# Norm scale and offset applied in the copy out of PSUM instead of being folded into the next weights

## The chip, the cores and the metric

The kernel runs on one core of one Trainium2 chip. The time is device microseconds of one execution; the time before is the median of three runs, 3001.75 us (2999.12 to 3003.61). A profile was taken of one further execution, whose own time was 3113.44 us and whose span from the first to the last instruction was 3111.6 us. All durations below come from that profiled execution, which is 3.7% longer than the runs.

Engine names in the profile: PE is the matrix engine, PEld its weight loads, DVE the vector engine, ACT the scalar (activation) engine, POOL the engine that issues the indirect DMAs (gathers and scatters of rows), SP the engine that issues plain DMAs.

## The reference

Eight graphs share one sparse adjacency matrix of 2048 nodes (a node has about 16 neighbours). Each node has 128 features. Four layers run one after the other. Layers 0 and 1 are transformer layers with attention over the neighbours; layers 2 and 3 are graph attention (GAT) layers. Cut to what matters:

```python
# layers 0 and 1
Q, K, V = h @ Wq, h @ Wk, h @ Wv
attn = softmax(where(adj == 0, -inf, Q @ K.T / sqrt(16)))      # per head, 8 heads of 16
x = layer_norm(h + attn @ V @ Wo + bo) * ln1_g + ln1_b
y = relu(x @ W1 + b1) @ W2 + b2
x = layer_norm(x + y) * ln2_g + ln2_b
# layers 2 and 3
h = x @ W
e = leaky_relu(h @ a_src [rows] + h @ a_dst [columns], 0.2)
x = layer_norm(softmax(where(adj == 0, -inf, e)) @ h + x) * ln_gamma + ln_beta
```

Every layer norm has a scale (g) and an offset (b) of 128 numbers each.

## The kernel before

**Tiling and stages.** Nodes are sorted by their number of neighbours and cut into 16 blocks of 128 nodes. A block has as many neighbour places per node as its largest node needs (30 for the first block, 11 for the last). For each place the kernel gathers one table row per node by an indirect DMA on POOL (L323): a row of layers 0 and 1 holds K and V of all 8 graphs, a row of layers 2 and 3 holds h of all 8 graphs and, behind it, the two exponentials of each graph's score (the *factors*). Layer l works on the table of layer l, which the layer before has written block by block (`put_rows`, L511). The span has these parts, by where the scatters of L511 and the first product of each layer lie: a start (0 to 170 us: reading the adjacency, sorting, table 0, preparing weights), layer 0 (to about 1200 us), layer 1 (to 2056), layer 2 (to 2658), layer 3 (to the end).

**One chunk.** In layers 0 and 1 a chunk is two places: DVE multiplies the gathered K by q (L658), adds halves of heads (L663), PE transposes and sums the heads into scores (L330 into `pair`), ACT takes the exponential (L676), PE turns it back, DVE multiplies V by the weights (L692), and PE adds the rows up through transposes (L330 into `acc`). In layers 2 and 3 a chunk is up to four places: DVE forms the weights (L820 to L827) and multiplies seven of eight graphs by them (L832), ACT the eighth (L837), and PE adds up into `acc`.

**The tail of a block.** When a block's sums are there, `attention_tail` (two halves of four graphs each) or `gat_tail` takes them through the norm and the products of the layer. PE forms the residual and the layer's output in one PSUM tile, with the mean removed by centred weights; ACT squares with a running sum (L490, L879), takes the root by Ln and Exp, scales (L497, L887); PE transposes the result (L337), ACT copies it to SBUF (L761, L795, L894). The copy is the layer's state x without its norm's scale and offset. Then `project` forms the rows of the next layer's table: PE multiplies the state by the next layer's weights, ACT copies to `rows`, and when both halves are done `state_done` saves the state (SP) and scatters the rows (POOL).

**Where scale and offset are.** In the kernel before they are folded at the start: `prepare` multiplies the next weights by the scale (L240, L282), makes copies of the centring matrix times the scale for the residuals (`residual`, L253), and turns offset times weights into rows of bias (`fold`, L236 to L241; `parts`, L220 to L231, splits a row in three bf16 parts so that a bf16 product of ones with it gives it back in full precision). Each product in the tails then begins with one such bias product on PE, of 512 columns: in `project` for layer 1 (L524), in `project` for layers 2 and 3 (L538, and L548 of eight columns for the scores), for q in `attention_begin` (L592), and in `gat_tail` (L865). Those of L744 and L777 in `attention_tail` are for bo and b2 and exist for themselves.

**GAT projection.** `project` for layers 2 and 3 takes two PSUM tiles: one for h of four graphs (L544: four products of 128 columns) and one for their scores (L553: four products of 2 columns with the same stationary operands). An f32 product is two passes on PE, so each shows as two instructions. After one `yield` ACT copies h (L558), takes three exponentials of four columns (L561 to L563) and copies the scores (L564).

**Order of the work.** The order is written out by hand. Tails and other side work are generators; each `yield` hands back, and `slot` advances every one of them by a step, three times per chunk (`slot`, L1175). `fetch` (L1151) issues gathers ahead of the chunks, into six buffers, so a gather waits until PE has added up the chunk that held its buffer. Gathers and scatters share POOL's queue in program order. A new layer starts when enough blocks of its table are put (L1160). Near a layer's end `hurry` advances the tails by a fourth step in three slots. `misc` gives PSUM tiles out of a pool of three in rotation; each new one waits for the readers of the third before it. `prepare` is advanced four times in the start's loop (L1055), twice at its end (L1099, L1100), and run out at L1235.

Of the kernel before, what the change touches and what calls it, by code (L numbers as in the profile page):

```python
# [17 lines left out]
P = 128  # L18
# [66 lines left out]
def sparse_path(ctx: ExitStack, tc: tile.TileContext, ins: dict, out: bass.AP, flag: bass.AP):  # L85
# [19 lines left out]
    def misc():  # L105
        return pm.tile([P, 512], F32, tag="m", name="m")
# [53 lines left out]
    score = const.tile([P, 2, NT, 2 * B], F32, name="score")  # L160
# [42 lines left out]
    W[0]["bias"] = None  # L203
    for l in (2, 3):
        W[l] = {
            "h": const.tile([P, D + 2], F32, name=f"w_L{l}_h"),
            "T": load(f"L{l}_wt", [P, D]),
            "col": load(f"L{l}_col", [P, 4]),
            "row": row(f"L{l}_row", D),
        }  # L210
        nc.scalar.dma_start(W[l]["h"][:, :D], ins[f"L{l}_gnn_W"])
# [21 lines left out]
    def fold(w, gain, offset_col, columns):  # L233

        pr = pair
        nc.tensor.matmul(pr[:1, :columns], offset_col, w[:, :columns], start=True, stop=True)  # L236
        yield
        r = line(columns)
        nc.vector.tensor_copy(r, pr[:1, :columns])
        nc.vector.tensor_scalar_mul(w[:, :columns], w[:, :columns], gain)  # L240
        return r  # L241

# [8 lines left out]
    def residual(gain, k):  # L251
        t = const.tile([P, P], F32, name=f"res_{k}")
        nc.vector.tensor_scalar_mul(t, center, gain)  # L253
        return t

    def prepare():

        gain = offset = offset_row = None
        for l in (0, 1):
            w = W[l]  # L260
            w["res1"] = center
            row_z = w["row"][:, 0, :]
            if gain is not None:
                r = yield from fold(w["qkv"], gain, offset, 384)
                nc.vector.tensor_scalar_mul(r[:, :D], r[:, :D], 0.25)
                w["bias"] = parts(r, f"qkv{l}")
                w["res1"] = residual(gain, f"1_{l}")
                nc.vector.tensor_add(row_z, row_z, offset_row)
            nc.vector.tensor_scalar_mul(w["qkv"][:, :D], w["qkv"][:, :D], 0.25)
            centered(w["o"])  # L270
            centered(row_z)
            w["row_z"] = parts(row_z, f"z{l}")
            g1, b1 = w["col"][:, 0:1], w["col"][:, 1:2]
            pb = pair
            for f in range(2):
                nc.tensor.matmul(
                    pb[:, f : f + 1], w["1"][:, f * P : (f + 1) * P], b1, start=f == 0, stop=f == 1,
                    skip_group_check=True,
                )
            yield  # L280
            nc.vector.tensor_add(w["col"][:, 4:6], w["col"][:, 4:6], pb[:, :2])
            nc.vector.tensor_scalar_mul(w["1"], w["1"], g1)  # L282
            for f in range(2):
                centered(w["2"][:, f, :])
            w["res2"] = residual(g1, f"2_{l}")
            row_y = w["row"][:, 1, :]
            nc.vector.tensor_add(row_y, row_y, w["row"][:, 2, :])
            centered(row_y)
            w["row_y"] = parts(row_y, f"y{l}")
            gain, offset, offset_row = w["col"][:, 2:3], w["col"][:, 3:4], w["row"][:, 3, :]  # L290
        for l in (2, 3):
            w = W[l]
            pa = pair
            nc.tensor.matmul(pa[:, :2], w["T"], w["col"][:, 2:4], start=True, stop=True)
            yield
            nc.vector.tensor_copy(w["h"][:, D : D + 2], pa[:, :2])
            centered(w["h"][:, :D])
            w["bias"] = parts((yield from fold(w["h"], gain, offset, D + 2)), f"h{l}")
            w["res1"] = residual(gain, f"1_{l}")
            centered(offset_row)  # L300
            w["row_z"] = parts(offset_row, f"z{l}")
            gain, offset, offset_row = w["col"][:, 0:1], w["col"][:, 1:2], w["row"]

# [195 lines left out]

    def clear_late():  # L500

        rows = rows_of(blocks[0][0])
        nc.vector.memset(rows, 0.0)
        for l in (1, 2, 3):
            for t in range(NT - 3, NT):
                for _ in range(3):
                    yield
                put_rows(l, t, rows)
# [8 lines left out]
    def project(l, i, xT, rows, t):  # L517

        w = W[l]
        if l < 2:  # L520
            for h in range(0, 4, 2):
                pp = misc().rearrange("p (b c) -> p b c", c=2 * D)
                if w["bias"] is not None:
                    nc.tensor.matmul(  # L524
                        pp, ones_bf, w["bias"][:, None, D:].to_broadcast([P, 2, 2 * D]),
                        start=True, stop=False, skip_group_check=True,
                    )
                for j in range(2):
                    nc.tensor.matmul(
                        pp[:, j, :], xT[:, i + h + j, :], w["qkv"][:, D:],  # L530
                        start=w["bias"] is None and j == 0, stop=True, skip_group_check=True,
                    )
                yield
                at = (i + h) * 2 * D
                nc.scalar.copy(rows[:, at : at + 512], pp.rearrange("p b c -> p (b c)"))
        else:
            pp = misc().rearrange("p (b c) -> p b c", c=D)
            nc.tensor.matmul(  # L538
                pp, ones_bf, w["bias"][:, None, :D].to_broadcast([P, 4, D]),
                start=True, stop=False, skip_group_check=True,  # L540
            )
            ps = misc()[:, :8].rearrange("p (b c) -> p b c", c=2)
            for j in range(4):
                nc.tensor.matmul(  # L544
                    pp[:, j, :], xT[:, i + j, :], w["h"][:, :D],
                    start=False, stop=True, skip_group_check=True,
                )
            nc.tensor.matmul(  # L548
                ps, ones_bf, w["bias"][:, None, D:].to_broadcast([P, 4, 2]),
                start=True, stop=False, skip_group_check=True,  # L550
            )
            for j in range(4):
                nc.tensor.matmul(  # L553
                    ps[:, j, :], xT[:, i + j, :], w["h"][:, D:], start=False, stop=True,
                    skip_group_check=True,
                )
            yield
            nc.scalar.copy(rows[:, i * D : (i + 4) * D], pp.rearrange("p b c -> p (b c)"))  # L558

            at = NB * D + i  # L560
            nc.scalar.activation(rows[:, at : at + 4], ps[:, :, 0], AF.Exp)  # L561
            nc.scalar.activation(rows[:, at + NB : at + NB + 4], ps[:, :, 0], AF.Exp, scale=SLOPE)
            nc.scalar.activation(own[:, t, i : i + 4], ps[:, :, 1], AF.Exp, scale=SLOPE - 1)  # L563
            nc.scalar.copy(score[:, l - 2, t, 2 * i : 2 * i + 8], ps.rearrange("p b c -> p (b c)"))  # L564
# [14 lines left out]
    def attention_begin(l, t, box):  # L579
# [9 lines left out]
        for i in range(0, NB, 4):  # L589
            pq = misc().rearrange("p (b c) -> p b c", c=D)  # L590
            if wt["bias"] is not None:
                nc.tensor.matmul(  # L592
                    pq, ones_bf, wt["bias"][:, None, :D].to_broadcast([P, 4, D]),
                    start=True, stop=False, skip_group_check=True,
                )
            for j in range(4):
                nc.tensor.matmul(
                    pq[:, j, :], xT[:, i + j, :], wt["qkv"][:, :D],
                    start=wt["bias"] is None and j == 0, stop=True, skip_group_check=True,
                )  # L600
            yield
            nc.scalar.copy(q[:, i : i + 4, :], pq)
# [135 lines left out]
    def attention_tail(l, t, box, i):  # L738
# [9 lines left out]
        for j in range(4):  # L748
            nc.tensor.matmul(
                z[:, j, :], xT[:, i + j, :], wt["res1"], start=False, stop=False,  # L750
# [10 lines left out]
        nc.scalar.copy(n1T, pt)  # L761
# [19 lines left out]
        for j in range(4):  # L781
            nc.tensor.matmul(
                y[:, j, :], n1T[:, j, :], wt["res2"], start=False, stop=False,
# [11 lines left out]
        nc.scalar.copy(xT[:, i : i + 4, :], pt)  # L795
# [54 lines left out]
    def gat_tail(l, t, box):  # L850
# [12 lines left out]
        def added(h):  # L863
            ys[h] = y = misc().rearrange("p (b c) -> p b c", c=D)
            nc.tensor.matmul(  # L865
                y, ones_bf, wt["row_z"][:, None, :].to_broadcast([P, 4, D]),
                start=True, stop=False, skip_group_check=True,
            )
            for j in range(4):
                turn_into(y[:, j, :], box["o"][:, 4 * h + j, :], False)  # L870
                nc.tensor.matmul(  # L871
                    y[:, j, :], xT[:, 4 * h + j, :], wt["res1"], start=False, stop=True,
# [16 lines left out]
        def half_rows(h):  # L889
# [4 lines left out]
            nc.scalar.copy(xT[:, 4 * h : 4 * h + 4, :], pt)  # L894
# [210 lines left out]
    def verdict():  # L1105
        ok = small.tile([P, 5], F32, tag="ok", name="ok", bufs=1)
        nc.vector.tensor_sub(over[:, 0, :], every_sum, kept_sum)
        every = score.rearrange("p a t b -> p (a t b)")
# [714 lines left out]
```

## Time and profile before

| what | us |
|---|---|
| median of three runs | 3001.75 |
| the profiled execution | 3113.44 |
| its span | 3111.6 |
| PE busy | 2636.0 (85%) |
| DVE busy | 2578.9 (83%) |
| ACT busy | 1345.7 (43%) |
| POOL busy | 1769.9 (57%) |
| moved by DMA | 987.71 MB, 317 GB/s |

The granted PE clock has a mean of 0.916 over the span. A group's busy time is the union of its instructions; matmuls are pipelined, so a group's mean duration (some 280 ns for 128 columns) is longer than the distance at which the next one follows. The chain of waits shows that distance, because there each piece ends where the next begins. The page's chain reaches back to about 1187 us only, the middle of the change from layer 0 to layer 1; its shares are shares of the whole span.

### The profile page before, as it was taken

Reading aid. Unit: us, or ns where it says so; the run is one execution under the profiler, and the core shown is the slowest. Engines: PE = TensorE matmul, PEld = TensorE weight load, DVE = VectorE, ACT = ScalarE, POOL = GpSimd, SP = SyncE. Lnnn points to the kernel's source line nnn. Section 1 sums busy time; section 2 is a strip of 40 time slices with the busy share of each in tenths; the row PEclk is TensorE's granted clock in tenths of the full one; section 3 lists DMA queues with packets and bytes.
Section 4 is the critical chain, followed back from the end, with each engine's and each line's share of the span. In section 5 each row is a group of like instructions: output and inputs, shape, how many; then the busy total and the mean of one; then the engine's idle time right before and its main releaser. Section 6 shows DMA issues by size and latency. Waiting matters only on the chain.

```text
span 3111.6 us, 53258 instructions
## 1 busy us (share of the span) xinstructions
PE 2636.0 (85%) x19620; PEld 2357.3 (76%) x19620; DVE 2578.9 (83%) x2633; ACT 1345.7 (43%) x4989; POOL 1769.9 (57%) x1296
## 2 busy tenths in 40 slices
PE   5867899989999996899899999986778888678886
PEld 3656778877888885788788888875767778577776
DVE  8898989988989878989888889865878786578886
ACT  3512344434555551334443545553444455144354
POOL 0257677688566445455455564644666563566663
PEclk8978999999999998999999999998888889888898
DMA  8788888998999777798888898867889997999994
GB/s 326 254 340 334 319 307 331 334 332 324 337 353 333 283 284 297 268 360 320 313 320 342 316 324 331 321 219 263 332 333 349 347 334 258 336 338 372 365 365 183
DMA packets 200698, 987.71 MB, mean 317 GB/s; under 512 B 31918, under 2 KB 33712, under 8 KB 128436
## 3 DMA queue, kind: packets, MB, share of 16 engines
q0 software_dynamic: 175024, 890.45, 77.1%
q1 hardware_dynamic: 20502, 75.52, 6.5%
q10 hardware_dynamic: 4904, 18.24, 1.5%
q8 instruction: 159, 2.61, 0.3%
q14 instruction: 109, 0.89, 0.1%
HBM read 937.16 MB, written 91.55 MB: 331 GB/s over the span
## 4 chain that ended last, share of the span: by engine, by line
PE 34%; issue 8%; DVE 7%; DMA 5%; ACT 4%; POOL 2%; another core or an unknown queue 2%; POOLq 0%; DVEq 0%; ACTq 0%
PE acc L330 14%; DMA kv<-table,lists 4%; PE pair L330 2%; POOL kv L323 2%; DVE kv L658 2%; DVE kv L692 2%; PE m L337 2%; PE m L766 2%; PE m L787 2%; PE m L544 2%; ACT n L879 2%; PE m L553 2%; PE m L330 1%; PE m L871 1%
## 5 line engine op out<-in xcount | busy, mean ns | idle before, releaser
L323 POOL DMA_INDIRECT kv<-table,lists x955 | 1313.7, 1376 | 888.2 <-PE acc L330 425.8
L330 PE MATMUL acc<-ident,kv 128*128 128x128 f32 x8208 | 1114.5, 289 | 172.9 <-issue 78.6
L330 PEld LDWEIGHTS acc<-ident,kv 128*128 128x128 f32 x8208 | 996.2, 150 | 251.9 <-issue 136.8
L658 DVE TENSOR_TENSOR kv<-kv,q 128x2048 f32<-128x2048 f32 (+1 forms) x282 | 630.1, 2234 | 145.1 <-DMA kv<-table,lists 95.8
L692 DVE TENSOR_TENSOR kv<-kv,weights 128x2048 f32<-128x2048 f32 (+1 forms) x284 | 634.1, 2233 | 30.9 <-ACT weights L684 26.5
L832 DVE TENSOR_TENSOR kv<-kv,pair 128x3584 f32<-128x3584 f32 (+1 forms) x150 | 540.1, 3601 | 2.3 <-DVE ws L826 0.4
L330 PE MATMUL pair<-ident,hk 128*128 128x128 f32 (+1 forms) x2272 | 309.1, 281 | 109.2 <-DVE hk L663 106.2
L663 DVE TENSOR_TENSOR hk<-kv 128x1024 f32<-128x1024 f32 (+1 forms) x284 | 340.4, 1199 | 28.8 <-DVE kv L658 0.9
L330 PEld LDWEIGHTS pair<-ident,hk 128*128 128x128 f32 (+1 forms) x2272 | 264.0, 144 | 129.2 <-issue 101.3
L676 ACT ACTIVATE eT<-pair 128x128 f32<-128x128 f32 (+1 forms) x284 | 78.3, 276 | 451.2 <-PE pair L670 422.4
L323 POOL DMA_INDIRECT kv<-table,sorted_lists x153 | 187.9, 1228 | 120.1 <-PE pair L680 35.9
L490 ACT ACTIVATE n<-m,eps 128x128 f32<-128x128 f32 x512 | 181.5, 372 | 163.0 <-PE m L787 147.8
L684 ACT COPY weights<-pair 128x128 f32<-128x128 f32 (+1 forms) x284 | 74.0, 261 | 395.7 <-PE pair L680 338.8
L879 ACT ACTIVATE n<-m,eps 128x128 f32<-128x128 f32 x256 | 90.6, 371 | 328.7 <-PE m L871 101.9
L837 ACT ACTIVATE kv<-kv,ws 128x128 f32<-128x128 f32 x554 | 176.6, 402 | 93.2 <-DVE ws L826 60.7
L511 POOL DMA_INDIRECT table<-rows,perm x57 | 92.7, 1627 | 140.0 <-ACT score L564 39.7
L787 PE MATMUL m<-w_L_w,hT 128*128 128x128 f32 x1024 | 157.1, 276 | 0.0
L497 ACT ACTIVATE n<-m,rs 128x128 f32<-128x128 f32 x512 | 145.9, 375 | 0.1
L766 PE MATMUL m<-n1T,w_L_gnn_W 128*128 128x512 f32 x256 | 134.7, 610 | 7.1 <-issue 5.2
L843 DVE TENSOR_TENSOR kv<-kv 128x1024 f32<-128x1024 f32 x75 | 91.6, 1221 | 56.8 <-ACT kv L837 56.6
L787 PEld LDWEIGHTS m<-w_L_w,hT 128*128 128x128 f32 x1024 | 135.9, 193 | 0.0
L337 PE MATMUL m<-ident,n 128*128 128x128 f32 x640 | 116.9, 299 | 22.2 <-ACT n L887 6.9
(252 smaller groups left out, 4053.2 us busy)
## 6 DMA issues: line engine op xcount, KB each, us to landing
kept<-xT SPq DMA_DIRECT2D x48, 512.0 KB
xT<-kept SPq DMA_DIRECT2D x48, 512.0 KB
kv<-in_adj_dram SPq DMA_DIRECT2D x16, 1024.0 KB
table<-kv ACTq DMA_DIRECT2D x16, 1024.0 KB
kv<-table,lists POOLq DMA_INDIRECT x955
kv<-in_x_nodes_dram SPq DMA_DIRECT2D x16, 512.0 KB
kv<-table,sorted_lists POOLq DMA_INDIRECT x153
found<-cand POOLq DMA_DIRECT2D x16, 64.0 KB
```

Source lines behind the costliest of these rows:

```text
L323: nc.gpsimd.indirect_dma_start(out=dst, out_offset=None, in_=tables[l][:, :], in_offset=bass.IndirectOffsetOnAxis(ap=index, axis=0), bound ...
L330: nc.tensor.matmul(dst, src, ident, start=start, stop=True, is_transpose=True, skip_group_check=True)
L337: nc.tensor.transpose(pt[:, j * P : (j + 1) * P], src[:, j, :], ident)
L490: nc.scalar.activation(dst[:, i, :], z[:, i, :], AF.Square, bias=eps, scale=D**-0.5, accum_out=ss[:, i : i + 1],)
L658: nc.vector.tensor_mul(kk, kk, q[:, None].to_broadcast([P, ns, NB, D]))
L663: nc.vector.tensor_add(hk.rearrange("p j (c h) -> p c j h", h=NH), kj[:, :, :NH, :], kj[:, :, NH:, :])
L692: nc.vector.tensor_mul(vv, vv, w.rearrange("p (s b h) -> p (s b) h", b=NB, h=NH)[:, :, None, :] .to_broadcast([P, ns * NB, HD, NH]),)
L766: nc.tensor.matmul(ph, wt["1"][:, f * P : (f + 1) * P], n1T.rearrange("p b c -> p (b c)"), start=True, stop=True,)
L787: nc.tensor.matmul(y[:, j, :], hT[:, f, j, :], wt["2"][:, f, :], start=False, stop=f == 1, skip_group_check=True,)
L832: nc.vector.tensor_mul(hv[:, :, :nv, :], hv[:, :, :nv, :], wc[:, :, :nv, None].to_broadcast([P, ns, nv, D]))
L837: nc.scalar.mul(hv[:, i, b, :], hv[:, i, b, :], ws[:, i, b - nv : b - nv + 1])
L879: nc.scalar.activation(ns[h][:, j, :], ys[h][:, j, :], AF.Square, bias=eps, scale=D**-0.5, accum_out=ss[:, j : j + 1],)
```

## The change

Scale and offset of a norm are applied where ACT copies the transposed state out of PSUM: the plain copy becomes an activation `Identity(scale * x + bias)`, with one scale and one bias per partition (a feature is a partition there). The state then is the finished x; the folded weights, the five scaled centring matrices and the bias products of L524, L538, L548, L592 and L865 go, with the code that prepares them. The last layer's scale and offset (L917, L919) stay as they are.

`project` for layers 2 and 3 now works in two steps of two graphs each: one product of 130 columns per graph gives h and both scores together, in one PSUM tile; ACT copies h and then the scores, and after each step's products there is a `yield`. The exponentials are taken once per block, for all eight graphs, from the saved scores, when both halves are there.

```diff
+    projected = {}
@@ prepare(): fold() and residual() are removed @@
         for l in (0, 1):
             w = W[l]
-            w["res1"] = center
-            row_z = w["row"][:, 0, :]
-            if gain is not None:
-                r = yield from fold(w["qkv"], gain, offset, 384)
-                nc.vector.tensor_scalar_mul(r[:, :D], r[:, :D], 0.25)
-                w["bias"] = parts(r, f"qkv{l}")
-                w["res1"] = residual(gain, f"1_{l}")
-                nc.vector.tensor_add(row_z, row_z, offset_row)
             nc.vector.tensor_scalar_mul(w["qkv"][:, :D], w["qkv"][:, :D], 0.25)
             centered(w["o"])
+            row_z, row_y = w["row"][:, 0, :], w["row"][:, 1, :]
             centered(row_z)
             w["row_z"] = parts(row_z, f"z{l}")
...
-            nc.vector.tensor_add(w["col"][:, 4:6], w["col"][:, 4:6], pb[:, :2])
-            nc.vector.tensor_scalar_mul(w["1"], w["1"], g1)
+            yield
             for f in range(2):
                 centered(w["2"][:, f, :])
-            w["res2"] = residual(g1, f"2_{l}")
...
+            yield
         for l in (2, 3):
...
             centered(w["h"][:, :D])
-            w["bias"] = parts((yield from fold(w["h"], gain, offset, D + 2)), f"h{l}")
-            w["res1"] = residual(gain, f"1_{l}")
-            centered(offset_row)
-            w["row_z"] = parts(offset_row, f"z{l}")
...
+    def affine(dst, src, col):
+        nc.scalar.activation(dst, src, AF.Identity, scale=col[:, 0:1], bias=col[:, 1:2])
@@ project(l, i, xT, rows, t): the new body @@
         w = W[l]
+        wide = 2 * D if l < 2 else D + 2
+        for h in range(i, i + 4, 2):
+            pp = misc()[:, : 2 * wide].rearrange("p (b c) -> p b c", c=wide)
+            for j in range(2):
+                nc.tensor.matmul(
+                    pp[:, j, :], xT[:, h + j, :], w["qkv"][:, D:] if l < 2 else w["h"],
+                    start=j == 0, stop=True, skip_group_check=True,
+                )
+            yield
+            if l < 2:
+                nc.scalar.copy(
+                    rows[:, h * wide : (h + 2) * wide], pp.rearrange("p b c -> p (b c)")
+                )
+            else:
+                nc.scalar.copy(
+                    rows[:, h * D : (h + 2) * D].rearrange("p (b c) -> p b c", c=D), pp[:, :, :D]
+                )
+                nc.scalar.copy(score[:, l - 2, t, h : h + 2, :], pp[:, :, D:])
...
+        projected[l, t] = projected.get((l, t), 0) + 1
+        if projected[l, t] == 2:
+
+            at = NB * D
+            both = score[:, l - 2, t]
+            nc.scalar.activation(rows[:, at : at + NB], both[:, :, 0], AF.Exp)
+            nc.scalar.activation(rows[:, at + NB : at + 2 * NB], both[:, :, 0], AF.Exp, scale=SLOPE)
+            nc.scalar.activation(own[:, t, :], both[:, :, 1], AF.Exp, scale=SLOPE - 1)
@@ attention_begin: the bias product of L592 is removed; attention_tail: @@
-                z[:, j, :], xT[:, i + j, :], wt["res1"], start=False, stop=False,
+                z[:, j, :], xT[:, i + j, :], center, start=False, stop=False,
...
-        nc.scalar.copy(n1T, pt)
+        affine(n1T, pt, wt["col"][:, 0:2])
...
-                y[:, j, :], n1T[:, j, :], wt["res2"], start=False, stop=False,
+                y[:, j, :], n1T[:, j, :], center, start=False, stop=False,
...
-        nc.scalar.copy(xT[:, i : i + 4, :], pt)
+        affine(xT[:, i : i + 4, :], pt, wt["col"][:, 2:4])
@@ gat_tail @@
-            nc.tensor.matmul(
-                y, ones_bf, wt["row_z"][:, None, :].to_broadcast([P, 4, D]),
-                start=True, stop=False, skip_group_check=True,
-            )
             for j in range(4):
-                turn_into(y[:, j, :], box["o"][:, 4 * h + j, :], False)
+                turn_into(y[:, j, :], box["o"][:, 4 * h + j, :], j == 0)
                 nc.tensor.matmul(
-                    y[:, j, :], xT[:, 4 * h + j, :], wt["res1"], start=False, stop=True,
+                    y[:, j, :], xT[:, 4 * h + j, :], center, start=False, stop=True,
                     skip_group_check=True,
                 )
...
-            nc.scalar.copy(xT[:, 4 * h : 4 * h + 4, :], pt)
+            affine(xT[:, 4 * h : 4 * h + 4, :], pt, wt["col"][:, 0:2])
```

## The prediction

> **What bounds the kernel now.** I read the busy times by stage first, then the chain of waits in each stage, then the groups of the lines that go. The windows below are the start (two parts), layers 0, 1, 2 and 3; the columns after the stage's length are busy us and instructions of each engine, the granted PE clock, the DMA engines' busy share and GB/s.
>
> ```profile
> core 0: us, PE busy (x) PEld busy (x) DVE busy (x) ACT busy (x) POOL busy (x), PEclk, DMA share, GB/s
> 0.00:135.00 135.00, 89.25 (x436) 70.18 (x436) 120.57 (x441) 62.83 (x151) 22.95 (x32) 0.92 0.83 313
> 135.00:170.00 35.00, 20.53 (x84) 14.86 (x84) 21.45 (x105) 8.59 (x16) 8.92 (x9) 0.76 0.50 153
> 170.00:1200.00 1030.00, 920.88 (x6983) 812.54 (x6983) 910.30 (x717) 442.14 (x1553) 669.45 (x404) 0.95 0.88 328
> 1200.00:2056.00 856.00, 785.49 (x6188) 703.04 (x6189) 739.49 (x452) 369.44 (x1440) 459.38 (x270) 0.96 0.83 310
> 2056.00:2658.00 602.00, 469.94 (x3320) 434.12 (x3319) 443.74 (x504) 276.67 (x1097) 339.21 (x317) 0.83 0.85 314
> 2658.00:3112.00 454.00, 349.91 (x2613) 322.60 (x2611) 343.39 (x419) 186.06 (x734) 270.00 (x266) 0.87 0.88 327
> ```
>
> The start is DVE's (121 of 135 us). Layers 0 and 1 have PE at 89 and 92%, DVE at 88 and 86%, the DMA engines at 83 to 88%: three resources near their end. Layers 2 and 3 have PE and DVE at 74 to 78% and a lower clock. ACT has room everywhere. The chain of waits decides which one is paid for. Its pieces, added up by stage (from 1187 us, where it begins), give PE 543, DVE 145, DMA 79 and ACT 8 of 869 us in layer 1; PE 321, ACT 76, issue 70, DMA 66, DVE 35 of 602 in layer 2; PE 180, issue 97, ACT 51 of 454 in layer 3. So PE is the main term, and in layer 2 the lines to be removed stand on the chain itself (start, us, what):
>
> ```profile
> 2297.01 0.58 ACT xT L894
> 2297.58 0.04 issue
> 2297.63 2.08 PE m L544 x8
> 2299.70 0.01 PE m L548
> 2299.71 1.71 PE m L553 x8
> ...
> 2306.77 0.22 PE m L538
> 2306.99 0.89 PE m L544 x8
> 2307.88 0.01 PE m L548
> 2307.88 0.89 PE m L553 x8
> 2317.18 0.21 PE m L865
> ```
>
> The reader is to see that the score products of two columns (L553) take as long as those of 128 columns (L544): 0.89 us for eight passes, 0.111 us each, at full clock; at the low clock 1.7 to 2.1 us. A bias product of 512 bf16 columns (L538, L865) takes 0.22 us.
>
> **PE, removed.** Per half of a block, `project` for layers 2 and 3 loses L553 (0.89), L538 (0.22) and L548 (about 0.01 on the chain); the h products grow from 128 to 130 columns, eight passes by 0.111 x 2/128 = 0.01, nothing. `gat_tail` loses one L865 (0.22), layer 1's `project` two L524 per half and its queries one L592 (0.22 each, by L538). With 32 halves per layer, at full clock: layer 0 64 x 0.22 = 14.1 us (L524); layer 1 32 x (0.22 + 0.89 + 0.22) = 42.6 (L592 and `project` for layer 2); layer 2 32 x (0.89 + 0.22 + 0.22) = 42.6, more at its clock; layer 3 7.0. Together 106 us.
>
> Not all of it is on the path. The chain holds, of these lines, 28.3 us in layer 1 (L553 17.0, L592 7.2, L538 4.1: two thirds of 42.6), 42.8 in layer 2 (L553 31.4, L538 6.0, L865 5.4: all of it, at the low clock), and 4.4 of 7.0 in layer 3. Layer 0 has no chain; like layer 1, two thirds of 14.1, 9.4. Sum 85 us. When these pieces go, the next wait ends: in layers 0 and 1 DVE's multiplications, in layer 2 the gathers and DVE. I take the same two thirds again, because in layer 1 that is the share of PE's work that ends last against the same rivals: 57 us. The bounds are 85 (nothing else comes up) and 17, a fifth (in layers 0 and 1 DVE and DMA take all of it, in layer 2 half goes to waits for gathers).
>
> **DVE at the start, removed.** The weights' folding in the first 75 us is 54.02 to 58.51 (4.5 us) and two times 0.83 us (L281, L282, L253, L287): 6.1 us, on a DVE that is never idle there from 37 us on. The adjacency it reads comes by DMA, 88% busy in that stretch, but no wait for it is seen after 27.7 us, so I take all 6.1 (bounds 2 and 6.1). Then the neighbour lists of block 0 (L374), which release the first gather, stand behind the folding for layer 2:
>
> ```profile
> 149.73 0.28 DVE L239 COPY spare<-pair 1x130 f32<-1x130 f32 x1 [8.21 <-PE pair L236]
> ...
> 154.72 0.18 DVE L228 COPY parts_z<-spare 1x128 bf16<-1x128 bf16 x1
> 154.93 0.29 DVE L374 MAX8 top<-cand 128x8 f32<-128x128 f32 x1
> ```
>
> DVE still waits until 149.7, now for L294's product, which moves behind the same PE work (L529); then it has a copy and a centring, 0.86 us by their rows at 140.67 to 141.53, and not 5.2. That is 4.3 us. Layer 3's folding (161 to 168) lies under the first gather and counts nothing; without that cover it would be 5. The start gives 10.4 us.
>
> **ACT, added.** The 160 copies of 512 columns become activations with two pointer operands. One pointer costs 108 ns by the rows:
>
> ```profile
> L771 ACT ACTIVATE hT<-m,w_L_col 128x512 f32<-128x512 f32 x128 | 89.3, 698 | 6.4 <-PE m L337 6.4
> L761 ACT COPY n1T<-m 128x512 f32<-128x512 f32 x64 | 37.7, 589 | 0.0
> ```
>
> Two are not shown; between 108 (the second is free) and 216 I take 216, as the two look alike: 64 x 0.22 = 14 us in each of layers 0 and 1, 7 in layer 2. ACT is 2% of these copies' stages on layer 1's chain, while L894 has 5.4 of its 18.8 us on layer 2's: 0.3 + 0.3 + 2.0, some 3 us. If ACT had no room, 35. In `project` for layers 2 and 3 a half now has two copies of 256 columns (0.37 each, between 0.26 for 128 and 0.59 for 512), two score copies of 0.20, and half of three exponentials of 0.18: 1.42 us against 1.34 (L558 to L564). Nothing.
>
> That Identity needs no other table is assumed. The trace has one table load, although Relu, Square, Exp and Ln alternate. [...]
>
> **The extra step.** Each half of `project` for layers 2 and 3 has one more `yield`, so state and scatter are issued one slot later, and on POOL the scatter may fall behind a chunk's gathers (L323), which wait for PE to free a buffer (445 us in 243 waits, 1.8 us each). Within a layer nobody needs that table yet. At the two changes 1 to 2 and 2 to 3 the first gathers wait for it: a slot is 602/(75 chunks x 3) = 2.7 us, shorter when only tails run; between 0 and 2 x (2.7 + 1.8) = 9 I take 3. The exponentials now follow the score copy of the second half, which is ACT's own order and no new wait. Against it stands that `project` held two of the three PSUM tiles at once and now holds one; I count nothing, up to 10 us.
>
> **Sum.** 57 + 10.4 - 3 - 3 = 61 us of the profiled 3111.6. The runs are at 3001.75/3113.44 = 0.964 of that: 59 us, 2943 us.
>
> **A rule that speaks against it.** The clock rows read 0.83 in layer 2 and 0.87 in layer 3. [...] This kernel's PE work is mostly transposes, and the change removes true products: of layer 2's 3320 instructions true ones fall from 936 of 3320 (28%) to 544 of 2928 (19%). [...] But layer 3 has the fewest true products (288 in 2613, 11%) and the higher clock, and long runs of nothing but transposes go at 0.109 us each there (80 in 8.73 us on the chain). The row decides: no loss taken.
>
> **The rivals.**
>
> 1. Other resources take over what PE gives up: a fifth of the chain's 85, 17 us, and the start's 10: 27 - 3 = 24, times 0.964, 23 us: 2979. For it: DVE at 86 to 88% and DMA up to 99% in single stretches. Against: the chain of layer 2.
> 2. All of the chain's 85 us comes off, with the start and some of the PSUM tiles' relief: 85 + 10 + 3 - 6 = 92, 89 us: 2913.
> 3. Slower: [...]
> 4. The change does nothing to the time, because the gathers pace everything: 2998 to 3006. Against: POOL waits for PE to free buffers (445 us), so gathers follow PE.
>
> **How the numbers follow.** Forecast 2943 with chance 0.55 (its own range 2922 to 2968), rival 1 0.23, rival 2 0.14, rival 3 0.05, rival 4 0.03. The range 2902 to 2985 leaves out rivals 3 and 4 (0.08), a third of rival 1 above it and a third of rival 2 below: 0.2. 0.2% is about what a measurement of this kernel tells from no change; faster by more 0.92, within 0.03, slower 0.05.
>
> **What would show it.** Right: L553, L538, L548, L865, L524 and L592 gone; L544's successor at eight passes in about 0.9 us; layer 2 shorter by 25 to 35 us, layer 1 by about 20, layer 0 by 6; first L658 near 160 and not 170.6; ACT's copies near 0.8 us. Wrong: more idle DVE and PE in layer 2 with a clock below 0.80; DMA waits before L658 growing by what PE lost; table loads on ACT; a longer gap before the first gathers of layers 2 and 3.

## The result and the profile after

| | median us | lowest to highest | runs |
|---|---|---|---|
| before | 3002.68 | 2999.12 to 3007.17 | 4 |
| after | 2954.78 | 2951.35 to 2965.97 | 4 |

The ratio is 0.9846 [0.9816, 0.9877]: 47.9 us less by the medians, 46 by the ratio (37 to 55 by its interval), where 59 were forecast.

Layers 2 and 3 of the changed kernel take about 110 us longer on the chips of the experiments than in the runs above, and the profile shown of the kernel before is of that longer condition too; so each ratio below is taken against the kernel before on the same chip, and stages are compared between profiles of like length.

The stage windows of the changed kernel, on the chip of the result: the start up to the first product, now L597, and then layers 0 to 3. The columns are those of the windows shown for the kernel before: length, busy us and instructions of each engine, PE clock, DMA share, GB/s.

```profile
0.00:159.30 159.30, 106.91 (x506) 83.45 (x506) 126.19 (x475) 70.94 (x167) 31.61 (x42) 0.91 0.80 299
159.30:1189.60 1030.30, 920.82 (x6901) 814.65 (x6902) 911.00 (x717) 454.43 (x1552) 675.72 (x403) 0.94 0.87 328
1189.60:2026.70 837.10, 755.62 (x5901) 674.94 (x5900) 739.11 (x455) 388.28 (x1456) 454.63 (x272) 0.95 0.85 319
2026.70:2552.50 525.80, 392.20 (x2921) 367.23 (x2920) 440.45 (x501) 282.44 (x1115) 340.76 (x316) 0.88 0.91 356
2552.50:2955.50 403.00, 316.13 (x2584) 308.01 (x2582) 342.92 (x419) 187.08 (x734) 271.00 (x266) 0.91 0.92 368
```

The start ends at 159.3 instead of 170.6. Layer 0 is as long as before (1030), layer 1 is 19 us shorter. Layers 2 and 3 are 929 us together, against 1056 in the profile shown before; but this after-profile is an execution like its runs (2957.34 us), while the one of before was not (3113.44 us against 3002), so most of these 127 us are not the change's.

The like pair is `before_again`, the kernel before unchanged, and `after_again`, the changed kernel unchanged, profiled on two chips of the experiments (3137.51 and 3070.32 us, 67 apart). First before, then after, in the same columns:

```profile
0.00:170.40 170.40, 107.97 (x520) 84.17 (x520) 141.94 (x545) 72.02 (x167) 32.09 (x42) 0.89 0.76 280
170.40:1208.50 1038.10, 930.68 (x6981) 821.36 (x6981) 911.65 (x717) 443.18 (x1552) 656.29 (x404) 0.94 0.87 325
1208.50:2068.70 860.20, 784.32 (x6193) 701.42 (x6193) 739.13 (x452) 370.63 (x1442) 462.02 (x270) 0.96 0.83 308
2068.70:2671.70 603.00, 464.12 (x3326) 426.62 (x3326) 443.29 (x502) 276.12 (x1097) 335.09 (x317) 0.86 0.86 313
2671.70:3135.70 464.00, 354.58 (x2604) 327.35 (x2602) 343.01 (x419) 186.07 (x734) 269.90 (x266) 0.86 0.87 320
```

```profile
0.00:159.70 159.70, 105.28 (x506) 82.02 (x506) 126.19 (x476) 71.19 (x167) 31.96 (x42) 0.91 0.81 299
159.70:1197.70 1038.00, 923.58 (x6903) 816.34 (x6904) 911.84 (x717) 454.73 (x1552) 662.32 (x404) 0.94 0.87 325
1197.70:2030.50 832.80, 755.96 (x5897) 675.58 (x5896) 738.58 (x453) 388.14 (x1456) 458.81 (x272) 0.95 0.85 320
2030.50:2609.80 579.30, 420.86 (x2922) 383.00 (x2921) 443.07 (x502) 283.56 (x1114) 338.15 (x315) 0.84 0.87 323
2609.80:3068.50 458.70, 352.75 (x2584) 328.99 (x2583) 343.30 (x419) 186.13 (x734) 270.55 (x266) 0.84 0.87 323
```

The rows show where PE's work went and how much of the time followed it. In layer 0 PE is busy 7 us less and the time is the same; in layer 1 it is 28 us of work and 27 of time, in layer 2 43 and 24, in layer 3 2 and 5. DVE, POOL and the DMA share hardly move, and ACT has 12, 18 and 7 us more in layers 0 to 2.

The chain of waits tells what took PE's place in layer 2. Its pieces, added up by engine there: PE 297 before and 217 after, ACT 75 and 106, issue 75 and 90, DVE 43 and 66, DMA 64 and 65. So PE lost 80 us on the chain, and ACT, issue and DVE took 31, 15 and 23 of them back; waits for a queue that the profile doesn't know fell from 36 to 17. In layer 1 PE went from 508 to 441, DMA from 82 to 124, DVE from 144 to 134.

### The profile page after: what moved, and what is told of

Read it like the earlier page. It is cut to its first block, busy times and chain, and to the rows that moved or that the text cites. A ratio compares the mean times of both kernels' runs of the same rounds, so it can differ in the third digit from the quotient of the medians.

```text
span 2955.5 us, 51651 instructions
## 1 busy us (share of the span) xinstructions
PE 2491.7 (84%) x18806; PEld 2248.3 (76%) x18806; DVE 2559.7 (87%) x2563; ACT 1383.2 (47%) x5021; POOL 1773.7 (60%) x1296
## 5 line engine op out<-in xcount | busy, mean ns | idle before, releaser
L288 PE MATMUL acc<-ident,kv 128*128 128x128 f32 x8208 | 1090.8, 287 | 154.3 <-DVE kv L631 60.5
L597 DVE TENSOR_TENSOR kv<-kv,q 128x2048 f32<-128x2048 f32 (+1 forms) x282 | 630.0, 2234 | 142.6 <-DMA kv<-table,lists 107.0
L472 POOL DMA_INDIRECT table<-rows,perm x57 | 80.6, 1414 | 110.5 <-issue 18.4
L485 PE MATMUL m<-w_L_h,xT 128*128 128x130 f32 x512 | 84.0, 296 | 38.4 <-ACT xT L459 24.0
```

The source lines that it names most:

```text
L288: nc.tensor.matmul(dst, src, ident, start=start, stop=True, is_transpose=True, skip_group_check=True)
L597: nc.vector.tensor_mul(kk, kk, q[:, None].to_broadcast([P, ns, NB, D]))
```

## The experiments

The theory: the gain is PE's time on the chain, bias products and score products, plus 10 us at the start; ACT's new operands and the extra step cost a few us. The rivals: the time is held by another resource (the transfers, ACT's operands, DVE), or the gain is a matter of the profile's condition.

**The kernel before, profiled once more** (no edit). Was the 3113 us execution a stray one?

> The kernel before once more, for a second profile. Between the two profiles the start is 11 us shorter, layer 0 the same, layer 1 19 us shorter, and layers 2 and 3 together 126 us shorter (1055 to 929), while the runs differ by 48 us in all. My theory: the first profile of before was itself slower in layers 2 and 3 than its runs are, because its transfers were (314 to 327 GB/s, 357 to 367 in the kernel after). Then this profile should have a span near 3000 us, the start, layer 0 and layer 1 as in the first (170, 1030, 856), and layers 2 and 3 together near 945 to 950. The rival, that the profile shows the true layers 2 and 3 and the runs hide a loss elsewhere, expects 1055 again and a span near 3110.

Measured: 3137.51 us, and 27 runs of the kernel before beside it have a median of 3141.45 (3121 to 3158). Layers 2 and 3 are 1067 us together. My theory missed: the longer condition isn't a stray execution but what these chips do. Where it lies is seen in the changed kernel, which has a profile in each condition (the tables above): the start, layer 0 and layer 1 agree within 1%, layers 2 and 3 take 929 and 1038 us. What the prediction had scaled evenly over the span (0.964) sits in two stages.

**PE's work put back, all of it and in two parts.** From the changed kernel: `bias_back` begins the same products as before with a bias product (of zeros), `split_back` computes h and scores in separate tiles in one step, `both_back` does both. `split_back` and `both_back` so bring back the order of the old projection too: one step, two PSUM tiles, exponentials by halves. The copies on ACT keep scale and offset, and the start stays the new one.

```diff
 # bias_back: project for layers 1 to 3; likewise in attention_begin for l == 1 and in gat_tail
+            if l > 0:
+                nc.tensor.matmul(
+                    pp, ones_bf, no_bias[:, None, :wide].to_broadcast([P, 2, wide]),
+                    start=True, stop=False, skip_group_check=True,
+                )
 # split_back: project for layers 2 and 3
+            for j in range(4):
+                nc.tensor.matmul(
+                    pp[:, j, :], xT[:, i + j, :], w["h"][:, :D],
+                    start=j == 0, stop=True, skip_group_check=True,
+                )
+            for j in range(4):
+                nc.tensor.matmul(
+                    ps[:, j, :], xT[:, i + j, :], w["h"][:, D:], start=j == 0, stop=True,
+                    skip_group_check=True,
+                )
+            yield
```

> The kernel after with all of the removed PE work put back: bias products of zeros where L524, L538, L548, L592 and L865 stood, and the GAT projection in the old form (four products of 128 and four of 2 columns, one step, exponentials per half). The copies with scale and offset and the shorter start stay. If PE work is the cause of the gain outside the start, the time is the start's 11 us (and the added ACT time) from before: about 2990 to 2995. If the gain came from the order of the work (tiles of PSUM, steps) as much as from PE, also 2990, so the next two tell these apart. If the removal of PE work is hidden, 2955 to 2965.

> The kernel after with bias products of zeros put back in all places (in the GAT projection one of 260 columns per step of two graphs), all else as after. By my sum the bias products are worth 9.4 (layer 0) + 11.3 (layer 1) + 11.4 (layer 2) + 4.4 (layer 3) = 36 us on the chain, two thirds of it 24 us: 2975 to 2980. If DMA paces layers 2 and 3 and layer 0 gave nothing, as the stages say: layer 1 alone, 8 us: 2960 to 2965.

> The kernel after with the GAT projection in the old form without bias (four products of 128 columns and four of 2 columns, one step, exponentials per half). By my sum L553 is worth 17.0 (layer 1) + 31.4 (layer 2) = 48 us on the chain, two thirds of it 32 us: 2980 to 2990. If DMA paces layer 2: layer 1's 11 us and little more: 2963 to 2970.

| | us | ratio to before | of after_again's gain of 0.0208 it takes |
|---|---|---|---|
| both_back | 3136.23 | 0.9978 [0.9958, 0.9997] | 0.0186 |
| split_back | 3109.09 | 0.9898 [0.9858, 0.9938] | 0.0106 |
| bias_back | 3081.88 | 0.9805 [0.9770, 0.9841] | 0.0013 |

The three ran on one chip; `after_again`, reported next, ran on another.

With `both_back` the gain outside the start is gone: 0.0022 is left, 7 us of 3141, while the start alone is 11 shorter. So what the change adds on ACT costs about 4 us (between -2 and 10 by the interval), and some 58 us (0.0186 x 3141, with an uncertainty of 11) come from PE's work together with the order of the projection. `one_step` below puts the step and the tiles at 9 us, not told apart from nothing; the exponentials by halves were not tried alone. Most of the 58 us is therefore PE's work.

The two parts are unequal, and what each is worth depends on the other. The score products, 64 halves by 0.89 = 57 us of PE time, are worth 33 us when put back alone (0.0106 x 3141, with an uncertainty of 16 from the two intervals) and 54 (13) on top of the bias products, all with the old order. The bias products, by 0.22 us each on the chain, L524 14.1 + L592 7.0 + L538 14.1 + L865 14.1 = 49 us of PE time, are worth 4 (15) alone and 25 (14) on top of the score products. Alone on the same chip the two differ by 29 us (17), so the score products with their order are worth more; what the bias products are worth stays between nothing and some 25. Together they give 58: more than the 37 of the parts, by about as much as the intervals allow.

**The changed kernel again**, and **both products in one step**: `one_step` computes the 130-column products of all four graphs ahead of one `yield`, in two PSUM tiles, as the old `project` held two.

```diff
+            for h in range(i, i + 4, 2):
+                pp = misc()[:, : 2 * (D + 2)].rearrange("p (b c) -> p b c", c=D + 2)
+                pps.append(pp)
+                for j in range(2):
+                    nc.tensor.matmul(
+                        pp[:, j, :], xT[:, h + j, :], w["h"],
+                        start=j == 0, stop=True, skip_group_check=True,
+                    )
+            yield
```

> The kernel after as it is, beside the kernels above. In the last runs the kernel before took 3141 us and not 3002: layers 2 and 3 take some 1067 us there, as in the first profile of before[...]. If what each part takes off adds up, the time is 3082 + 3109 - 3136 = 3055 us, a ratio of 0.972: more than the 0.985 of the first comparison. If the gain is the same 48 us everywhere: 3093, 0.985.

> The kernel after with the GAT projection's products of both steps issued together and one yield, as before the change; two PSUM tiles held at once. I priced the extra step at a loss of 3 us (0 to 9), so this should be some 3 us faster than after. The rival, that holding one PSUM tile at a time and the shorter steps are worth more than the step costs, expects it 5 to 15 us slower than after.

`after_again` took 3063.89 us beside 3124.34 of the kernel before, 0.9792 [0.9761, 0.9823]: 60 us by the medians, 65 by the ratio (55 to 75), where the prediction's sum has 61 for this condition (0.9804). `one_step` took 3073.01, 0.9815 [0.9779, 0.9851]: 9 us more than `after_again`, not 3 less, and not told apart from it. A cost of the extra step isn't seen; if the two differ, the second PSUM tile costs more than the step.

**How much PE's work is worth further on**: `no_residual` leaves out the residual's products in the tails of layers 2 and 3 (64 halves, eight passes each by 0.111 us = 57 us of PE time, an estimate from the chain of the kernel before: two passes of L871 take 0.22 us at 2317.51, where the granted clock was 1.00), so its outputs lack the residual there.

```diff
                 turn_into(y[:, j, :], box["o"][:, 4 * h + j, :], j == 0)
-                nc.tensor.matmul(
-                    y[:, j, :], xT[:, 4 * h + j, :], center, start=False, stop=True,
-                    skip_group_check=True,
-                )
```

> The kernel after without the residual products in the tails of layers 2 and 3 (that part of the computation is left out): 32 halves x 8 passes x 0.111 us x 2 layers = 57 us less PE work at full clock, the same size as what the change took off in layers 1 and 2. If PE's work still ends last in layers 2 and 3: 25 to 45 us faster than after. If transfers pace them now: less than 12 us.

Measured: 3049.11 us, 0.9757 [0.9717, 0.9797], 15 us less than `after_again` by the medians and 11 by the ratios, with all four runs below all six of `after_again`; in the profiles layers 2 and 3 are 1020 instead of 1038. That is between the two expectations and nearer to the lower one: 57 us of PE time brought 11 to 18, a fifth to a third. After the change PE's work in layers 2 and 3 is worth less than the 56% (24 of 43) that it was worth in layer 2 before.

**The start**: `lists_first` no longer advances `prepare` ahead of the first lists, so L332 waits for no weight.

```diff
-        next(weights, None)
-        next(weights, None)
         for l in (2, 3):
```

> The kernel after without the two advances of the weights' preparation at the end of the start, so that the neighbour lists of block 0 no longer stand behind layer 2's score weights on DVE, whose product waits on PE behind 32 products of table 0. The preparation is run out after the first gathers are issued. Before, DVE idles 8.2 us there. Expected: first product of layer 0 some 4 to 6 us earlier than after's 159.3, and the time 4 to 6 us shorter. If the first gather is held by the lists' own transfer or by the last scatter of table 0, nothing.

Measured: 3060.63 us, 0.9787 [0.9754, 0.9821], and the first product at 158.8 instead of 159.7. DVE's instructions around the lists, in the timeline of `after_again` (start, us, engine, line, operation; in brackets the idle time before and what ended it):

```profile
141.88 0.16 DVE L260 COPY w_L_h<-pair 128x2 f32<-128x2 f32 x1 [8.46 <-PE pair L258]
...
142.66 0.29 DVE L332 MAX8 top<-cand 128x8 f32<-128x128 f32 x1
```

and in that of `lists_first`:

```profile
134.06 0.17 DVE L1026 TENSOR_TENSOR perm<-part,m 128x16 int32<-128x16 f32 x1
141.19 0.29 DVE L332 MAX8 top<-cand 128x8 f32<-128x128 f32 x1 [6.96 <-DMA cand<-found,perm]
```

The first product then waits 10.7 us for its gather in both. In the changed kernel the profile blames PE (8.46 us for L258's product). Without that wait the lists' own data (`cand`, a gather that needs `perm` at 134.2) arrives at 141.2, 1.5 us earlier than L332 ran. So most of the wait blamed on PE was covered by a transfer that came almost as late, and of the 4 to 6 us expected one came. By its runs `lists_first` is not told apart from the changed kernel.

**Are transfers the bound of layers 2 and 3?** Both kernels with rows of half the bytes there: the gathers fetch the factors, which stand first in the row now, and the h of four graphs; the h of the other four is left out, and their products read that of the first four.

```diff
     def gather(l, index, dst):
+        if l > 1:
+            dst = dst[:, : 2 * NB + 4 * D]
...
         for i in range(ns):
             for b in range(nv, NB):
-                nc.scalar.mul(hv[:, i, b, :], hv[:, i, b, :], ws[:, i, b - nv : b - nv + 1])
+                nc.scalar.mul(hv[:, i, b, :], hv[:, i, 0, :], ws[:, i, b - nv : b - nv + 1])
+        nc.vector.tensor_mul(
+            hv[:, :, 4:nv, :], hv[:, :, 1:4, :], wc[:, :, 4:nv, None].to_broadcast([P, ns, 3, D])
+        )
+        nc.vector.tensor_mul(
+            hv[:, :, :4, :], hv[:, :, :4, :], wc[:, :, :4, None].to_broadcast([P, ns, 4, D])
+        )
```

> The kernel before with half the bytes gathered in layers 2 and 3: the factors stand first in a table row, the gather takes them and the first four graphs, and the products of the other four graphs are formed from these four (so half of each row's values are left out); DVE's product is cut in two, PE and ACT do what they did. [...] If PE paces layers 2 and 3 of the kernel before (my reading of its chain): at most 40 us faster than before. If transfers pace them: 100 us and more.

> The same edit on the kernel after. The pair asks what took back the gain in layers 2 and 3. If transfers cap it, the two kernels with half the bytes differ in layers 2 and 3 by what the chain holds of the removed lines, 42.8 + 4.4 = 47 us, where with all bytes they differ by 29 us. If DVE, ACT and waits between engines cap it, they differ by 25 to 32 us as before, and half the bytes bring both kernels the same.

Both came out slower than the whole kernels: 3276.1 us, 1.0432 [1.0407, 1.0456], and 3284.06 us, 1.0449 [1.0424, 1.0474]. The list of waits in layers 2 and 3 (engine, line, what was waited for: us in total, times, longest) of `after_half` shows why:

```profile
DVE kv L779 <- ACT kv L775: 399.1, 81, 11.5
```

The edit made a wait of its own: DVE overwrites in place what ACT's product reads (`hv[:, i, 0, :]`), so it waits for ACT in chunk after chunk (in `before_half` 308.7 us, in 63 waits). Nothing follows about the transfers. The mended form, `half_free`, is the changed kernel with the same rows, ACT's product reading a constant tile instead:

```diff
-                nc.scalar.mul(hv[:, i, b, :], hv[:, i, b, :], ws[:, i, b - nv : b - nv + 1])
+                nc.scalar.mul(hv[:, i, b, :], center, ws[:, i, b - nv : b - nv + 1])
```

> The kernel after with half the bytes gathered in layers 2 and 3, mended: in the last two runs ACT's product read what DVE overwrites, so DVE waited for ACT (385 us), and the edit made the kernel slower by its own wait. Now ACT multiplies a constant tile in place of the eighth graph's values, and waits for nothing new (the values of four graphs and of the eighth are left out of the sums). Layers 2 and 3 of after took 1038 us in the last runs, at 320 to 356 GB/s. If transfers end last there after the change: 980 us or less, 60 us and more faster than after. If PE, DVE and ACT with the waits between them do: at most 25 us faster than after, with the DMA engines' busy share near 0.5.

Measured: 3054.14 us beside 3145.59, 0.9718 [0.9658, 0.9779]. Its windows of layers 2 and 3:

```profile
2031.00:2600.00 569.00, 414.16 (x2947) 378.11 (x2945) 455.42 (x581) 282.13 (x1111) 340.51 (x317) 0.86 0.65 192
2600.00:3054.00 454.00, 347.61 (x2526) 323.87 (x2526) 350.02 (x486) 184.99 (x730) 267.57 (x262) 0.84 0.63 181
```

The DMA share fell from 0.87 to 0.64 (not to the 0.5 expected) and GB/s from 323 to 187, and the two layers took 1027 us instead of 1038, though DVE's product, now in two, keeps DVE busy 19 us longer. On these chips transfers don't end last in layers 2 and 3; the engines and their waits do. The chain of `after_again` says the same: DMA has 65 of 579 us in layer 2 and 28 of 459 in layer 3. On the chip of the result the edit was not run.

**ACT's two operands**: `plain_copy` leaves scale and offset out of all 160 copies.

```diff
     def affine(dst, src, col):
-        nc.scalar.activation(dst, src, AF.Identity, scale=col[:, 0:1], bias=col[:, 1:2])
+        nc.scalar.copy(dst, src)
```

> The kernel after with plain copies in place of the 160 activations with scale and offset (scale and offset of the norms are left out; they are 1 and 0 in these inputs). An activation takes 785 ns, a copy 590. I priced the difference at 3 us in all, since ACT has room: 0 to 5 us faster than after. If ACT's latency is on the path of the tails, each of 160 at 0.195 us: up to 31 us faster.

Measured: 3065.99 us beside 3139.97, 0.9762 [0.9739, 0.9786]. That is 0.0030 below `after_again`, which ran on another chip: 9 us, with an uncertainty of some 12 from the two intervals. The operands cost no more than some 20 us, and may cost nothing.

## Why the prediction was right, and where it was off

**The time.** Inside the range and inside the forecast's own range (2922 to 2968). On the chips whose condition the sum was made for, 60 to 65 us came off where it had 61. On the chip of the result it was 46 to 48 where it had 59, and the weak step is the last one of the sum, the scaling by 0.964. It spread the difference between profile and runs evenly; that lies in layers 2 and 3, where 31 of the 61 us were to be won. That less came off on that chip is likely and not certain, as the intervals of the two ratios just overlap ([0.9761, 0.9823] and [0.9816, 0.9877]). Of the 48 us the start has 11, layer 1 19 to 23 (837.1 against 856.1 and 860.2), so 14 to 18 are left for layers 2 and 3 if layer 0 has none, against 29 in the like pair. I have no profile of the kernel before in that condition, so this part is worked out and not seen. What fits it is the list of waits in layers 2 and 3 of the changed kernel on the chip of the result,

```profile
ACT n L814 <- PE m L806: 184.2, 35, 12.0
ACT kv L776 <- DVE ws L765: 171.5, 43, 13.9
...
DVE kv L759 <- DMA kv<-table,lists: 47.3, 23, 19.6
...
DVE kv L759 <- DMA kv<-table,sorted_lists: 41.9, 15, 13.9
```

with 89 us of DVE's waits for gathers (55 in `after_again`), and its windows, where the DMA share is 0.91 and 0.92 with up to 413 GB/s in single slices of the page. The chain of waits of this profile reaches back to 2497 us, so it covers layer 3, and there transfers lead it: of 403 us DMA has 160 and PE 99, where `after_again` has DMA 28 and PE 258 of 459. Some of its pieces (start, us, what; shorter ones between them left out):

```profile
2673.85 8.72 DMA kv<-table,lists
2682.97 9.82 DMA kv<-table,lists
...
2706.10 6.11 PE acc L288 x56
```

So on that chip transfers are the largest item of what ends last in layer 3 after the change, as rival 1 had it; on the other chips PE is. For layer 2 this profile has no chain, and that transfers took the rest of the gain there is argued, not shown.

**PE, removed: size right, places off.** Two thirds of 85 = 57 us was to come off. The like pair has layer 0 at 0 (forecast 6), layer 1 at 27 (19, with 28.3 on the chain), layer 2 at 24 (28.5 less ACT's 2), layer 3 at 5 (3): 56. That the sum fits so well is partly luck: layer 1's 8 us too little and layer 0's 6 too much cancel. One factor for all layers was the weak step: in layer 1 nearly the whole chain came off, in layer 2 just over half. Layer 0's 6 us were carried over from layer 1 for want of a chain; the like pair shows nothing, but kernels whose layer 0 is one of these two lie between 1027 and some 1045 us there, so 6 can't be excluded. By the chain's pieces, two thirds of 48 = 32 us were to come from the scores and 24 from the bias products. Measured are 33 and 4 when each is put back alone, 54 and 25 on top of the other, each with an uncertainty of some 15: the scores brought what was forecast or more, and the bias products' part is not settled.

**Signs of being wrong.** The prediction named longer waits for gathers in layers 0 and 1 as one. DVE's idle time put down to gathers before the first product of a chunk (L658, now L597) went from 126 us to 139 in the like pair, so 13 us of waits came up there where PE lost 35 us of work: some of its gain, not all.

**The products themselves.** L485, of 130 columns, was to take eight passes in about 0.9 us, as L544 did. On the chain of the changed kernel, on the chip of the result, eight of them take 0.90 us (from 2514.81): right.

**The start.** 10.4 forecast, 10.7 and 11.3 measured. Its two terms: the lists' gather, issued when `perm` is there, starts 7.3 us earlier (134.3 for 141.6; forecast 6.1), the rest is 3.6 shorter (forecast 4.3). That DVE would still wait for L258's product (L294 before) was right, but by `lists_first` the lists' own transfer lies behind most of that wait.

**ACT.** The copies by form, in `after_again` (line, engine, operation, out<-in, count; busy us, mean ns of one; idle before):

```profile
L459 ACT ACTIVATE xT<-m,w_L_col 128x512 f32<-128x512 f32 x96 | 75.3, 785 | 11.2 <-PE m L295 9.1 <-remote 2.1
...
L495 ACT COPY rows<-m 128x256 f32<-128x256 f32 x128 | 47.8, 377 | 60.9 <-PE m L485 33.7 <-remote 10.8 <-PE acc L288 8.3
L498 ACT COPY score<-m 128x4 f32<-128x4 f32 x128 | 22.9, 179 | 0.0
```

785 ns for the 806 estimated from 590 + 2 x 108; 377 and 179 for the 0.37 and 0.20 of the two steps. Their cost on the path, 3 us forecast, is 4 (-2 to 10) by `both_back`, with the old order of the projection in it, and 9 with an uncertainty of 12 by `plain_copy`. There is still one table load on ACT in the whole kernel, of 1.3 us: the 160 activations with Identity brought none, as was assumed.

**The extra step and the PSUM tiles.** 3 us of loss and nothing of gain were taken; `one_step` differs by 9 us the other way, within what the runs scatter. Both stay unresolved and small.

**The granted clock.** On the chain of the kernel before, the eight passes of L544 (four f32 products, shown as x8) took 2.08 us where the granted clock was 0.50 (2297 to 2302 us) and 0.89 where it was 1.00 (2305 to 2309). In layers 2 and 3 the clock did fall from 0.86 to 0.84 in the like pair, but `both_back`, with all the true products back, has 0.84 in both too:

```profile
2068.30:2681.20 612.90, 473.71 (x3332) 433.26 (x3330) 442.53 (x502) 282.81 (x1096) 340.55 (x317) 0.84 0.85 308
2681.20:3148.20 467.00, 355.59 (x2599) 326.59 (x2597) 343.24 (x419) 185.71 (x734) 270.47 (x266) 0.84 0.87 318
```

So the drop can't be put down to the removed products; the same changed kernel has 0.88 and 0.91 on the chip of the result, and layer 2 became 24 us shorter in the like pair. That fewer true products would lower the clock, and with it the slower time of rival 3, was the author's estimate, and no run shows it; no loss was taken for it, and none is seen.

## What to carry to other kernels

A product's price on PE is worth its time only where the chain of waits holds it, and then by a share that differs from stage to stage: here nearly all in one layer (27 of 28 us), half in the next (24 of 43); use the chain of each stage and not one factor. If two pieces of work are taken out, put back each and both: alone the bias products looked worth 4 us, on top of the score products 25. If the profiled execution is longer than the runs, find out in which stage it is longer before the sum is scaled, because that stage may have another bound in the runs (here layer 3 of the changed kernel, with DMA at 160 of 403 us of the chain in one condition and 28 of 459 in the other). When an experiment reuses data to save transfers, look first at who writes it in place.

## What the runs showed of the hardware that was not expected

The 110 us that layers 2 and 3 take more on some chips show as idle time of PE, ACT and the weight loads that no semaphore of this core explains ("issue", and "remote" for another core or an unknown queue). In these layers PE's idle time put down to "issue" adds up to 112 us in the first profile of the kernel before, 140 in the second, 119 in `after_again` and 2 in the profile of the changed kernel on the chip of the result; ACT's idle time put down to "remote" adds up to 132, 105, 146 and 0. In layers 0 and 1 both are alike (PE's issue: 2 us). The list of waits in layers 2 and 3 of `after_again` begins with it:

```profile
ACT n L814 <- remote: 118.5, 9, 18.6
PEld acc L288 <- issue: 116.5, 139, 4.1
```

In its timeline the weight loads come in fours with a pause of 1 us between, every 1.4 us, and the first four of these take 0.42:

```profile
2289.28 0.42 PEld L288 LDWEIGHTS acc<-ident,kv 128*128 128x128 f32 x4 [1.05 <-issue]
2290.70 0.72 PEld L288 LDWEIGHTS acc<-ident,kv 128*128 128x128 f32 x4 [1.00 <-issue]
```

What makes them pause, why in these layers, and why on one chip and not on another, was not tried and stays open.
